# Layer 0's key layer norm: factor and shift on ScalarE in place of two-scalar instructions on VectorE, from the second quarter of keys on

## The chip, the core and the metric

The kernel runs on one core of one Trainium2 chip, in one launch. The core has five engines that work through queues of their own, each in order: TensorE (PE; its weight loads are shown as PEld), VectorE (DVE), ScalarE (ACT), GpSimd (POOL) and SyncE (SP), which here only issues DMAs. ACT issues some DMAs too. An instruction that has to wait holds up everything behind it on its engine. The metric is the device time of one execution in microseconds (us); lower is better.

## The reference, cut to what matters

The model has four blocks (a cross attention and a feed-forward net each) over `x`, 32 batches of 64 tokens of width 128, with a context `ctx_1024` of the same shape. The change lies in the first attention, layer 0, which has 16 heads of width 64:

```python
def _L0_xattn_ref(image_embeds, latents, ln1_g, ln1_b, ln2_g, ln2_b, Wq, Wkv, Wo):
    x = layer_norm(image_embeds, ln1_g, ln1_b)
    l = layer_norm(latents, ln2_g, ln2_b)
    q = l @ Wq
    kv_in = jnp.concatenate([x, l], axis=1)
    k, v = jnp.split(kv_in @ Wkv, 2, axis=-1)
    ...
    w = softmax(einsum('bhqd,bhkd->bhqk', q * scale, k * scale))
    ...
x = x + _L0_xattn_ref(ctx_1024, _layernorm(x, axis=-1), L0_xattn_ln1_g, ...)
```

Each batch has 128 keys: 64 context tokens and 64 latent tokens. A context row is normalised once; a latent row twice in a row, which the kernel does with one mean and one combined factor.

## The kernel before

**Layer 0.** The 32 batches are worked off in eight quarters `q` of four batches. `l0_load` (line 389) brings the keys of a quarter into a tile `kv_tok` of 128 partitions (rows 0 to 63 context, 64 to 127 latents) by four batches by 128, with one DMA on SP's queue and one on ACT's. There are two such buffers, so the load of quarter q+2 waits until quarter q has let go of its own.

`l0_inputs` (line 392) makes the keys ready. DVE takes mean and variance of every row (bn_stats and bn_aggr, lines 154 and 155) and adds the epsilon (lines 398 and 399, 64 rows each); POOL raises the result to the power -1/2 (line 161, tile `ln_rstd`); DVE applies it in place, one instruction of 128x128 for each of the four batches, with mean and factor as two per-partition scalars (`ln_apply`, line 183); then gain and bias rows are multiplied and added over the whole tile (lines 403 and 404), for quarter 0 on DVE and for the others on POOL. PE transposes the result (line 408), ACT copies it out of PSUM as `kvT` (line 409), and DVE and POOL split `kvT`'s latent half and `kv_tok` into a high and a low part (`latT`, `tokp`, lines 213 and 218).

`l0_project` (line 416) multiplies a quarter's latents with the folded query-key matrix A, in eight steps `n` of six matmuls (line 236); ACT copies each out as G (line 425). Its PSUM tag `g` has one bank. `l0_unit` (line 428) is the attention of one batch and eight heads: scores (line 445), maximum and subtraction on DVE (447, 451), exponential on ACT (452, or 456 in every eleventh), sum on DVE (453), reciprocal (460), scaling on POOL (461), transposes on PE (465), copies as high and low part (`pT_hi` on ACT, line 468; `pT_lo` on DVE, 469), the product with the keys (line 236) into `Ct` (ACT, line 473), and after the last unit of a 128-token tile the output product with N (line 479) and the addition to x (DVE, line 480).

**The order of the work.** `interleave` (line 382) runs 64 units with a depth of three, started in turn; between their steps it issues tasks from a list: first `mid_weights`, which loads and prepares weights of the next blocks (among them `w1e` and `w2e`, with large casts on ACT, line 213), then for each finished group of two quarters `mid_group` (layer 0's feed-forward net and layer 1's attention) and the first steps of layer 1's experts. A unit at `n == 0` issues the load of quarter q+2, at `n == 2` its `l0_inputs`. Quarters 0 and 1 are prepared at the start. This is the order of issue; a list scheduler in the compiler then orders each engine's instructions, so a change of one instruction can reorder others. After layer 0, about 320 us into the span, come the experts of layer 1, then layers 2 and 3; nothing of the change is there.

The lines of the change:

```python
    ln_apply(K, tok, tok, mv, rsqrt(K, gp, rs, "ln_rstd"))
    full = [P, GT, P]
    engine = nc.vector if q == 0 else nc.gpsimd
```

Of the kernel before, what the change touches and what calls it, by code (L numbers as in the profile page):

```python
# [23 lines left out]
AF = mybir.ActivationFunctionType  # L24
ALU = mybir.AluOpType
# [5 lines left out]
GT = 4  # L31
# [41 lines left out]
def bank(K, tag, shape, dt=F32):  # L73
    if tag == "c":
        K.cturn = not K.cturn
        tag = "c2" if K.cturn else "c1"
    if tag == "1":
        tag = "c1"
    if tag == "2":
        tag = "c2"  # L80
    return K.ps.tile(shape, dt, tag=tag, name=f"{tag}_ps", bufs=BANKS[tag])
# [65 lines left out]
def ln_moments(K, pool, xg, own=""):  # L147

    nc = K.nc
    n = xg.shape[1]  # L150
    st = pool.tile([P, n, 6], F32, name="ln_st")
    mv = pool.tile([P, n, 2], F32, name=f"ln_mv{own}")
    for t in range(n):
        nc.vector.bn_stats(st[:, t, :], xg[:, t, :])
        nc.vector.bn_aggr(mv[:, t, :], st[:, t, :])
    return mv


def rsqrt(K, pool, v, name):
    out = pool.tile(list(v.shape), F32, name=name)  # L160
    K.nc.gpsimd.tensor_tensor(out, v, K.neghalf.to_broadcast(list(v.shape)), ALU.pow)  # L161
    return out
# [18 lines left out]
def ln_apply(K, out, xg, mv, rstd, after=None):  # L181
    for t in range(xg.shape[1]):
        step = K.nc.vector.tensor_scalar(
            out[:, t, :], xg[:, t, :], mv[:, t, 0:1], rstd[:, t : t + 1], ALU.subtract, ALU.mult
        )
        if after:
            in_turn(K, [after, step])
    return step
# [19 lines left out]
def split(K, pool, src, name, engine=None, bufs=None, after=None):  # L208

    nc = K.nc  # L210
    hi = pool.tile(list(src.shape), F32R, name=f"{name}_hi", bufs=bufs)
    lo = pool.tile(list(src.shape), F32R, name=f"{name}_lo", bufs=bufs)
    first = nc.scalar.copy(hi, src) if isinstance(K, Later) else nc.vector.tensor_copy(hi, src)
    if after:
        in_turn(K, [after, first])
    if not isinstance(K, Later):
        K.mark = first
    (engine or nc.gpsimd).tensor_tensor(lo, src, hi.bitcast(F32), ALU.subtract)
    return hi, lo
# [111 lines left out]
def l0_xattn(K):  # L331
# [3 lines left out]
    with (  # L335
# [8 lines left out]
        with tc.tile_pool(name="first", bufs=1, side="right", reuse_waits="tile") as first:  # L344
# [16 lines left out]
            def take_A(ps, hf, r):  # L361
# [3 lines left out]
                nc.vector.scalar_tensor_tensor(lo, ps, scale, hi.bitcast(F32), ALU.mult, ALU.subtract)  # L365

            l0_inputs(K, C, 0)
            for hf in range(2):
                l0_products(K, take_A, w["WqT"], w["WkT"], hf)
                for n in range(4 * hf, 4 * hf + 4):  # L370
                    l0_project(K, C, 0, n, "gn"[n % 2])
            l0_inputs(K, C, 1)

            with tc.issue_after(K.projected.ins):
# [17 lines left out]
def l0_inputs(K, C, q):  # L392

    nc, gp = K.nc, C.gp
    tok = C.tok[q]
    mv = ln_moments(K, gp, tok)
    rs = gp.tile([P, GT], F32, name="ln_rs")
    nc.vector.tensor_scalar(rs[0:S, :], mv[0:S, :, 1], EPS, None, ALU.add)
    nc.vector.tensor_scalar(rs[S:P, :], mv[S:P, :, 1], 1.0 + EPS, EPS * EPS, ALU.mult, ALU.add)
    ln_apply(K, tok, tok, mv, rsqrt(K, gp, rs, "ln_rstd"))  # L400
    full = [P, GT, P]
    engine = nc.vector if q == 0 else nc.gpsimd
    engine.tensor_tensor(tok, tok, K.kv_gamma.unsqueeze(1).to_broadcast(full), ALU.mult)
    engine.tensor_tensor(tok, tok, K.kv_beta.unsqueeze(1).to_broadcast(full), ALU.add)
    kvT = gp.tile(full, F32, name="kvT", bufs=3)
    ps = bank(K, "1", full)
    for b in range(GT):
        nc.tensor.transpose(ps[:, b, :], tok[:, b, :], K.ident)
    nc.scalar.copy(kvT, ps)
    latp = split(K, gp, kvT[:, :, S : 2 * S], "latT", nc.vector)  # L410
    tokp = split(K, gp, tok, "tokp", bufs=3)
    C.keys[q] = (kvT, latp, tokp)
# [15 lines left out]
def l0_unit(K, C, q, t, hf, b):  # L428
# [8 lines left out]
    if n == 2 and q + 2 < 8:  # L437
        l0_inputs(K, C, q + 2)
# [941 lines left out]
def in_turn(K, steps):  # L1380

    for a, b in zip(steps, steps[1:]):
        order = mybir.DependencyInfo(mybir.DependencyClass.NoSync, mybir.DependencyReason.DATA)
        K.tc.add_manual_dep(b.ins, a.ins.name, order, reason="order of issue")
# [354 lines left out]
```

## Time and profile before

| what | value |
|---|---|
| median of 3 runs | 907.06 us (906.3 to 908.6) |
| the profiled execution | 907.62 us |
| its span | 905.9 us, 1.7 us less |
| mean granted TensorE clock | 0.98 |
| PE busy | 821.4 us (91%) |
| weight loads busy | 671.2 us (74%) |
| DVE busy | 732.4 us (81%) |
| ACT busy | 563.0 us (62%) |
| POOL busy | 328.3 us (36%) |

The profile is that of one execution. Its page gives busy time by engine, then the span in 40 equal slices of 22.6 us with the busy share of each in tenths, and the costliest groups of instructions. Further views are asked of its trace: busy time by window, what an engine waited for (put down to the instruction that came last), the instructions that read or write one tile, groups by form (shapes and operands), a timeline, and the chain of waits that ended last. Starts are counted in us from the start of the span. An instruction's duration reaches into that of its successor on the same engine, so the distance of two starts is less than the duration. The start of the span to about 18 us is loading and the first quarter; there PE has little to do.

### The profile page before, as it was taken

Reading aid. Unit: us, or ns where it says so; the run is one execution under the profiler, and the core shown is the slowest. Engines: PE = TensorE matmul, PEld = TensorE weight load, DVE = VectorE, ACT = ScalarE, POOL = GpSimd, SP = SyncE. Lnnn points to the kernel's source line nnn. Section 1 sums busy time; section 2 is a strip of 40 time slices with the busy share of each in tenths; the row PEclk is TensorE's granted clock in tenths of the full one; section 3 lists DMA queues with packets and bytes.
Section 4 is the critical chain, followed back from the end, with each engine's and each line's share of the span. In section 5 each row is a group of like instructions: output and inputs, shape, how many; then the busy total and the mean of one; then the engine's idle time right before and its main releaser. Section 6 shows DMA issues by size and latency. Waiting matters only on the chain.

```text
span 905.9 us, 15766 instructions
## 1 busy us (share of the span) xinstructions
PE 821.4 (91%) x5859; PEld 671.2 (74%) x5868; DVE 732.4 (81%) x1877; ACT 563.0 (62%) x1093; POOL 328.3 (36%) x300
## 2 busy tenths in 40 slices
PE   4999999999999988899999799898999779898995
PEld 3989989979988876787787688684676447566663
DVE  5879799798698687877678877789788778789878
ACT  3676685676676599587687768564544484345443
POOL 3764574343243251511040310015474303435342
PEclk9999999999999999999999999999999999899998
DMA  8312000000000000000000000000000000000000
GB/s 191 106 36 59 13 2 12 13 1 1 13 1 1 1 13 0 15 14 21 1 1 1 1 1 1 0 25 1 1 2 1 1 1 1 1 1 1 13 13 24
DMA packets 22670, 13.73 MB, mean 15 GB/s; under 512 B 3009, under 2 KB 21953, under 8 KB 22593
## 3 DMA queue, kind: packets, MB, share of 16 engines
q1 hardware_dynamic: 18320, 10.62, 4.3%
q10 hardware_dynamic: 4272, 2.10, 0.9%
q8 instruction: 46, 0.75, 0.3%
q14 instruction: 32, 0.25, 0.1%
HBM read 11.66 MB, written 1.05 MB: 14 GB/s over the span
## 4 chain that ended last, share of the span: by engine, by line
PE 50%; DVE 25%; ACT 15%; POOL 3%; issue 3%; DMA 2%; SPq 1%; ACTq 0%; DVEq 0%; POOLq 0%
PE c_ps L918 7%; PE g_ps L479 4%; PE s_ps L1263 4%; PE s_ps L445 4%; PE g_ps L236 4%; PE c_ps L236 3%; PE g_ps L1283 2%; PE c_ps L1273 2%; PE s_ps L236 2%; PE t_ps L465 2%; PE t_ps L236 2%; ACT L941 2%; DVE mh_lo L895 1%; ACT L936 1%; DVE m L893 1%
## 5 line engine op out<-in xcount | busy, mean ns | idle before, releaser
L461 POOL TENSOR_TENSOR e<-e,rs 128x512 f32<-128x512 f32 x64 | 67.0, 1058 | 91.7 <-DVE rs L460 52.8
L161 POOL TENSOR_TENSOR ln_rstd<-ln_rs,neghalf 128x4 f32<-128x4 f32 (+1 forms) x38 | 40.8, 1073 | 144.8 <-DVE ln_rs L169 137.5
L1249 POOL TENSOR_TENSOR kb<-hk,head 128x1024 f32<-128x1024 f32 x32 | 63.7, 1993 | 74.2 <-PE s_ps L1263 58.9
L445 PE MATMUL s_ps<-kvT,G 128*128 128x128 f32 x512 | 71.7, 277 | 0.5 <-DVE e L451 0.5
L1263 PE MATMUL s_ps<-kb,hq 128*128 128x512 f32 x128 | 67.3, 609 | 2.1 <-ACT hq L1232 1.9
L445 PEld LDWEIGHTS s_ps<-kvT,G 128*128 128x128 f32 x512 | 65.8, 192 | 4.1 <-DVE e L451 1.9
L918 PE MATMUL c_ps<-mh_hi,w2e_hi 128*128 128x512 f32 x160 | 61.8, 426 | 4.5 <-ACT be L936 2.7
L479 PE MATMUL g_ps<-N,Ct 128*128 128x128 f32 x512 | 62.1, 276 | 1.1 <-ACT G L425 0.7
L479 PEld LDWEIGHTS g_ps<-N,Ct 128*128 128x128 f32 x512 | 60.1, 192 | 2.5 <-ACT G L425 1.3
L1266 ACT ACTIVATE e<-e 128x1024 f32<-128x1024 f32 x32 | 34.0, 1061 | 40.6 <-DVE e L1265 38.1
L1264 DVE TENSOR_REDUCE nm<-s_ps 128x8 f32<-128x512 f32 x64 | 43.7, 683 | 16.0 <-PE s_ps L1263 15.6
L1274 ACT COPY hpT<-c_ps 128x512 f32<-128x512 f32 x64 | 35.1, 589 | 34.2 <-PE c_ps L1273 33.9
L469 DVE TENSOR_TENSOR pT_lo<-t_ps,pT_hi 128x512 fp32r<-128x512 f32 x64 | 43.4, 683 | 13.5 <-ACT pT_hi L468 11.3
L918 PE MATMUL c_ps<-mh_hi,w2e_lo 128*128 128x512 f32 x160 | 51.9, 401 | 0.0
L895 DVE TENSOR_TENSOR mh_lo<-m,mh_hi 128x1024 fp32r<-128x1024 f32 x32 | 40.4, 1263 | 13.9 <-ACT mh_hi L894 12.9
L473 ACT COPY Ct<-c_ps 128x512 f32<-128x512 f32 x64 | 38.4, 600 | 21.2 <-PE c_ps L236 16.4
L918 PE MATMUL c_ps<-mh_lo,w2e_hi 128*128 128x512 f32 x160 | 49.4, 404 | 0.5 <-DVE mh_lo L895 0.5
L425 ACT COPY G<-g_ps 128x512 f32<-128x512 f32 x60 | 35.9, 598 | 21.4 <-PE g_ps L236 18.0
L452 ACT ACTIVATE e<-e 128x512 f32<-128x512 f32 x56 | 35.4, 638 | 20.8 <-DVE e L451 20.5
L1283 PEld LDWEIGHTS g_ps<-hv,hpT 128*64 128x64 f32 x1024 | 33.5, 137 | 19.3 <-issue 7.4
L447 DVE TENSOR_REDUCE nm<-s_ps 128x4 f32<-128x512 f32 x64 | 42.9, 679 | 5.0 <-PE s_ps L445 4.7
L468 ACT CAST pT_hi<-t_ps 128x512 fp32r<-128x512 f32 x64 | 38.1, 598 | 13.3 <-PE t_ps L465 7.3
(524 smaller groups left out, 2651.8 us busy)
## 6 DMA issues: line engine op xcount, KB each, us to landing
kv_tok<-in_x ACTq DMA_DIRECT2D x8, 128.0 KB, 3.3
kv_tok<-in_ctx SPq DMA_DIRECT2D x8, 128.0 KB, 2.9
x<-in_x SPq DMA_DIRECT2D x4, 256.0 KB, 8.3
ctx<-in_ctx SPq DMA_DIRECT2D x4, 256.0 KB, 3.4
w2e_raw<-in_L_ffn_expert_w SPq DMA_DIRECT2D x1, 768.0 KB, 4.4
out<-x SPq DMA_DIRECT2D x3, 256.0 KB, 2.3
WkT<-in_L_xattn_WkT ACTq DMA_DIRECT2D x2, 256.0 KB, 5.3
WqT<-in_L_xattn_WqT SPq DMA_DIRECT2D x2, 256.0 KB, 5.2
```

Source lines behind the costliest of these rows:

```text
L236: step = K.nc.tensor.matmul(ps, w[a], x[b], start=start and i == 0, stop=stop and i == 2)
L445: nc.tensor.matmul(ps[:, j, :], G[:, bb, h : h + 2, :].rearrange("p h s -> p (h s)"), kvT[:, bb, :], start=True, stop=True)
L447: K.mark = nc.vector.tensor_reduce(nm, ps, AX.X, ALU.max, negate=True)
L461: nc.gpsimd.tensor_tensor(e, e, rs.unsqueeze(2).to_broadcast([P, 4, P]), ALU.mult)
L469: nc.vector.tensor_tensor(lo, ps, hi.bitcast(F32), ALU.subtract)
L479: nc.tensor.matmul(ps, Ct[:, h, :], C.N[:, h, :], start=(h == 0), stop=(h == 15))
L895: nc.vector.tensor_tensor(lo, m, hi.bitcast(F32), ALU.subtract)
L918: nc.tensor.matmul(ps, K.w2p[part][:, 2 * n + i, cols], x[:, i, :, :], start=first, stop=last)
L1249: step = nc.gpsimd.tensor_tensor(kb, K.hk[C.i][g][:, :, t, :].unsqueeze(2).to_broadcast(full), K.head.unsqueeze(1).unsqueeze(3).to_broadca ...
L1263: nc.tensor.matmul(ps, hq[:, half, t, :, :].rearrange("p b s -> p (b s)"), kb[:, half, :, :], start=False, stop=True)
L1264: nc.vector.tensor_reduce(nm[:, heads], ps, AX.X, ALU.max, negate=True)
L1283: values = nc.tensor.matmul(po[b * S : (b + 1) * S, j, :, :].rearrange("p r d -> p (r d)"), pT[:, j, b * S : (b + 1) * S], K.hv[g][:, 2 * ...
```

## The change

For the quarters 1 to 7 the layer norm of the keys is written as a factor and a shift: (x - m) r = r x + (-m r). DVE computes the shift, one instruction of 128x4, into the tile that held the variances; ACT applies factor and shift, one activation of 128x128 for each of the four batches, with both as per-partition columns. Quarter 0 keeps its instructions.

```diff
-    ln_apply(K, tok, tok, mv, rsqrt(K, gp, rs, "ln_rstd"))
+    rstd = rsqrt(K, gp, rs, "ln_rstd")
+    if q == 0:
+        ln_apply(K, tok, tok, mv, rstd)
+    else:
+
+        shift = rs
+        nc.vector.scalar_tensor_tensor(shift, mv[:, :, 0], -1.0, rstd, ALU.mult, ALU.mult)
+        for t in range(GT):
+            nc.scalar.activation(tok[:, t, :], tok[:, t, :], AF.Identity, bias=shift[:, t : t + 1], scale=rstd[:, t : t + 1])
     full = [P, GT, P]
     engine = nc.vector if q == 0 else nc.gpsimd
```

So 28 of the 32 instructions of line 183 on `kv_tok` leave DVE, seven small ones come to it, and 28 activations come to ACT. ACT now waits for DVE's shift, and POOL's multiplication with the gain waits for ACT where it waited for DVE. No DMA is added or taken away; those that wait for a `kv_tok` buffer keep their places in the queues of SP and ACT.

## The prediction

> **What bounds the kernel now.** I read the page's busy slices first, to see which engine fills the stage of the change; layer 0 with the keys' layer norm is the first third, slices 1 to 14.
>
> ```profile
> PE   4999999999999988899999799898999779898995
> DVE  5879799798698687877678877789788778789878
> ACT  3676685676676599587687768564544484345443
> ```
>
> TensorE is at 9 from slice 2 to slice 15, VectorE at 7 to 9, ScalarE at 6 or 7. Then the table of windows: start and end, length, then busy us and instructions of PE, its weight loads, DVE, ACT and POOL, granted clock, DMA share, GB/s.
>
> ```profile
> 18.00:60.00 42.00, 40.68 (x282) 37.04 (x283) 34.51 (x94) 26.61 (x58) 30.08 (x24) 1.00 0.29 86
> 60.00:120.00 60.00, 58.50 (x456) 54.59 (x454) 51.00 (x134) 38.90 (x81) 31.05 (x30) 1.00 0.10 28
> 120.00:180.00 60.00, 59.60 (x473) 56.56 (x474) 49.52 (x133) 39.52 (x88) 27.27 (x25) 1.00 0.04 10
> 180.00:320.00 140.00, 134.66 (x1041) 123.07 (x1041) 112.35 (x301) 92.33 (x191) 48.67 (x46) 1.00 0.02 5
> ```
>
> From 18 to 180 us, where all the moved instructions lie, PE is busy 158.8 of 162 us at full granted clock. DVE is busy 135.0 and ACT 105.0, so ACT has room of 57 us. Pipelined matmuls cover each other's tails, so I asked the waits of the weight-load queue for what PE really stands still for (18 to 320 us; total, times, longest).
>
> ```profile
> PEld g_ps L236 <- DVE latT_hi L213: 3.5, 1, 3.5
> PEld g_ps L236 <- ACT G L425: 2.7, 6, 1.0
> PEld c_ps L236 <- ACT Ct L473: 2.6, 6, 1.3
> PEld s_ps L445 <- DVE e L451: 1.9, 5, 0.8
> PEld g_ps L479 <- ACT G L425: 1.3, 3, 0.9
> PEld c_ps L236 <- DVE pT_lo L469: 0.6, 1, 0.6
> ```
>
> The first is the start, ahead of the changed code. Of the rest of that answer, the lines released by DVE add up to 3.9 us, 2.3 of them before 180 us; the lines released by ACT to 10.5. PE in this stage waits more for evictions by the half-idle ACT than for the busy DVE, because ACT works its queue in order and each eviction is short and urgent. That decides my sign.
>
> **What goes from DVE.** Line 183 on kv_tok, 28 of its 32 instructions.
>
> ```profile
> L183 DVE TENSOR_SCALAR kv_tok<-kv_tok,ln_mv,ln_rstd x32: 319/340/1302, 7.4 to 154.4; 128x128 f32<-128x128 f32 x32
> 91.17 1.83 DVE L183 TENSOR_SCALAR kv_tok<-kv_tok,ln_mv,ln_rstd 128x128 f32<-128x128 f32 x4 [0.52 <-POOL ln_rstd L161]
> 93.66 0.50 PE L236 MATMUL c_ps<-pT_lo,tokp_hi 128*128 128x512 f32 x1 [0.38 <-DVE pT_lo L469]
> ```
>
> In the timeline, the seven runs of four start at 17.97, 24.34, 32.86, 41.92, 91.17, 124.24 and 153.65 us and last 1.12, 2.07, 1.91, 1.11, 1.83, 1.10 and 1.11 us: 10.3 us. A quiet run takes 1.11; the three long ones lie beside POOL instructions. In exchange comes one 128x4 scalar_tensor_tensor a quarter, absent from the trace; its nearest rows are the 64x4 tensor_scalar of line 399 (166 to 1043 ns, median 167) and the 128x4 reciprocal of line 460 (0.17 us). I take 0.17, so 1.2 us in all (7.3 at the worst). DVE is 9.1 us lighter, between 3.0 and 9.5.
>
> How much reaches PE? The chain of waits names kv_tok on DVE twice, at 17.97 and at 91.17. But at 91.17 a delay of 1.83 us cost PE 0.38 us (last line above): PE had other units' matmuls to do. The most that relief can give directly is all of the 2.3 us; I take half, 1.2. The wait for POOL's rstd does not go: the shift needs it too, on the same queue, with reductions and subtractions behind it (0.52 us in the line above, 3.0 us in four waits in all).
>
> **What ACT gets.** 28 activations of 128x128, SBUF to SBUF, with two per-partition columns, not in this form in the trace. Nearest rows by form, busy us and mean ns after the bar:
>
> ```profile
> L818 ACT ACTIVATE hr<-c_ps,cols 128x128 f32<-128x128 f32 x2 | 0.7, 368 | 0.0
> L602 ACT ACTIVATE c<-n_ps,c 128x512 f32<-128x512 f32 x3 | 2.1, 690 | 0.5 <-PE n_ps L600 0.5
> L583 ACT ACTIVATE y<-n_ps,cols 128x512 f32<-128x512 f32 x12 | 9.7, 807 | 0.0
> L229 ACT ACTIVATE ws_raw<-ws_raw 128x128 f32<-128x128 f32 x1 | 0.3, 293 | 0.0
> ```
>
> Line 818 has one column: 368. Line 583 has two, line 602 one, at equal size: a second column costs 117. So 485 ns each. Back to back they overlap by about 0.11 us (copies of 0.58 start 0.47 apart, from 42.97 to 43.43), so a run of four takes 3 x 0.375 + 0.485 = 1.61 us, and 28 take 11.3. Bounds: the row without columns, 293, gives 4 x 0.18 = 0.73 us a run; no overlap gives 1.94. I keep 1.61, since the column rows are the nearer kind. It is half as long again as the quiet DVE run it replaces.
>
> What is queued behind each run I read from the order of instructions of the two builds: in quarters 1, 2 and 5 a copy of G comes directly behind it (in quarter 2 the run is split in pairs around such copies), in 3 and 7 a pT_hi and then a G, in 4 the w1e_raw negation and then a G, in 6 an activation of the middle group. G's PSUM tag g has one buffer, so PE's next group of line 236 waits for that copy, and the exponentials and pT_hi further back hold up DVE. ACT idles 35% from 60 to 180 us, so a run of 1.61 us falls by 0.56 into idle time and pushes what follows by 1.05. PE has a group of 0.7 to 0.9 us to do before it needs the bank and the copy takes 0.6: cover of 0.2. So 0.85 us passes to PE where an eviction stands close behind, which I count for five of seven runs: 4.3 us. With the bounds: five times (0.47 - 0.2) = 1.4, and seven times (1.26 - 0.2) = 7.4.
>
> The new wait, ACT for the shift, is worst in quarter 2: its statistics wait for a load that lands at 21.45, its rstd ends at 24.3, and behind the first pair on ACT stands the G copy that ran at 23.06. It could run at about 25.1. PE loses little, since the N-products of line 326 and transposes fill the gap; I count that as one of the five. POOL's gamma and beta of quarter 1 move from behind DVE's run to behind ACT's; its second pass comes behind quarter 2's rstd instead of ahead of it, so quarter 3's two loads (on SP's and ACT's queues, waiting for that buffer) start some 3 us later than 25.59. Quarter 3's projections run tens of us later; I cost this at nothing, and at 1 us if a DVE wait for that load reaches PE. Order of issue differs up to PE row 669 of 2473 (middle group 2, about 315 us); after that it is the same but for one swapped pair, so what layer 0 wins or loses is carried to the end.
>
> **A rule against the change, and one for it.** The traced rows above have ACT dearer than DVE (1.61 estimated against 1.11). The Trainium skill, "ScalarE: Activation LUTs", section "Rules for kernel authors", tells authors to put adds and multiplies on VectorE, not ScalarE. By those rows and engine time alone the change loses 3.5 us (7 x 0.5), which is less than the 4.3 I count. On the other side the three runs beside POOL took 1.83 to 2.07 instead of 1.11. The skill's "GPSIMD Engine Reference", section "Specifications", says that GpSimd's SBUF interfaces are shared with VectorE and that DVE instructions in a two-port mode contend. By the quiet row alone the relief would be 7.8, by all seven it is 10.3. No run here yet shows whether ACT escapes it.
>
> **Sum.** The profiled execution took 907.62 (span 905.9 and 1.7 around it), 0.56 above the median of 907.06. 907.62 + 4.3 - 1.2 = 910.7 for such an execution, 910.1 for a median; I say 910.0. Bounds of this case in medians: 907.06 + 1.4 - 2.3 = 906.2 to 907.06 + 7.4 = 914.5.
>
> **Rivals.**
> *Relief reaches PE* (faster). ACT's room of 57 us swallows the runs; PE gets back the 2.3 us, and the freed DVE lets the middle groups' chains start earlier, so that part of PE's waits from 180 to 320 us goes: they total 11.8 us in that view, of which I give up to half. 907.1 - 2.3 = 904.8 down to 898.9; I name 902. For it: DVE has 10 of 20 us of the chain in 80:100 and in 180:200. Against it: no kv_tok on DVE after 155 us, and the 0.38 us above. It decides where less than 0.3 us a run passes to PE.
> *PE hides both* (the move does nothing to the end): 906 to 908.5. For it: PE at 59.6 of 60 us. Against: ACT's 10.5 us of holds.
> *The rearranged start collides.* The later quarter 3 loads and the weights w1e and w2e, whose large casts sit in ACT's queue among evictions (w2e_hi 1.47 us at 55.33, Ct behind it), meet the runs; each held Ct delays a 1.8 us group of line 479: 8 to 12 us over, 915 to 919.
>
> **Chances.** A measurement of this kernel tells about 0.3% (2.7 us) from no change: 904.3 and 909.8 are the limits. Forecast 0.45 (0.31 slower, 0.14 within); relief 0.27 (all faster); hiding 0.14 (within); collision 0.14 (slower). Slower 0.45, same 0.28, faster 0.27. Leaving out the lower 0.08 of the relief and the upper 0.06 of the collision, with its highest bound, the range is 900 to 916. The forecast's own range is 906.2 to 914.5.
>
> **What would show it.** Right: ACT rows of about 0.49 us in kv_tok, ACT some 10 us and DVE minus 9 us in 18:180, PE's waits on ACT's G and Ct grown from 10.5 us by some 4, DVE's from 3.9 to under 3, layer 0's last output about 3 us later. Wrong: runs on ACT that lie wholly in its idle time, waits on ACT no longer than before, or a PE that is done with layer 0 earlier. A row under 0.3 us would fail the price; a large difference after 320 us, the carrying.

## The result, and the profile after

The kernel after took 911.39 us (median of 22 executions, 905.96 to 916.73), the kernel before, run on the same chip between them, 906.84 us (22, 903.74 to 911.9). The ratio is 1.0051, with a 95% interval of 1.0037 to 1.0064: slower by 4.5 us. The profiled execution after took 908.46 us (span 906.7), 0.84 more than that of before, at nearly the same mean granted TensorE clock (0.981 and 0.980).

One number has to be known before the others are read. In this study the time follows the granted clock: within the kernels, fitted together, 4.3 us less for each 0.01 more of mean clock (two of the smaller sets, of eight executions each, show little of it). The 22 executions after had a mean clock of 0.9761. The 22 of before that were run between them have no clock on record; the 98 of before that have one, run beside the experiments, had 0.9789. At a common clock of 0.978 the means are 910.7 and 907.5 us. So, as an estimate from these figures, about 3.2 us of the 4.5 belong to the change, and about 1.2 to a lower clock, the reason of which these runs don't show. I give both kinds of numbers below.

The busy slices of the page after:

```profile
PE   4999989999999997899999799998999878898995
DVE  4779879798689767867678787788887788979878
ACT  3786775666766589596677777564544575445443
```

PE still stands at 9 nearly all through layer 0. The windows, with the columns as before (busy us and instructions of PE, weight loads, DVE, ACT, POOL):

```profile
18.00:60.00 42.00, 39.19 (x281) 35.60 (x281) 31.43 (x85) 30.49 (x73) 27.67 (x26) 1.00 0.30 86
60.00:120.00 60.00, 59.22 (x462) 55.29 (x461) 51.43 (x132) 42.17 (x87) 30.07 (x27) 1.00 0.10 28
120.00:180.00 60.00, 56.67 (x435) 51.77 (x434) 46.62 (x119) 39.78 (x91) 27.97 (x26) 1.00 0.03 10
180.00:320.00 140.00, 135.92 (x1052) 124.26 (x1051) 113.59 (x299) 92.33 (x191) 50.43 (x47) 1.00 0.01 3
```

The third line tells where the time went. Up to 120 us PE does 743 instructions (738 before); from 120 to 180 it does 435 (473 before) and is busy 2.9 us less. The weight loads' waits from 18 to 320 us (total, times, longest) name what stands there now:

```profile
PEld g_ps L236 <- DVE latT_hi L213: 3.5, 1, 3.5
PEld s_ps L453 <- DVE e L459: 3.1, 6, 0.9
PEld g_ps L236 <- ACT G L433: 3.1, 7, 1.0
PEld s_ps L453 <- ACT e L464: 2.6, 2, 1.5
PEld n_ps L588 <- ACT y L591: 2.1, 2, 1.9
PEld c_ps L236 <- ACT Ct L481: 2.0, 5, 1.0
```

Those released by ACT add up to 13.5 us (10.5 before), those by DVE, without the start, to 5.0 (3.9 before). Of the 10.5 before, only 3.8 lie ahead of 180 us, where the moved instructions are; there they have grown to 7.4. What has grown is not the copies: all lines of G and Ct together fell from 7.6 to 5.7 us (18 to 320 us). Two other lines are new among the large ones: `e` of line 464, the exponential of every eleventh unit (0.2 before, on line 456), and `y` of line 591, layer 0's feed-forward net in middle group 0 (0.7 before).

A ruler makes it sharper, if it is read with care: the starts of the 16 additions to x (line 480, now 488), one for each output tile of layer 0. In the table, starts in us in the profiled executions.

| output tile | 1 | 2 | 5 | 6 | 7 | 8 | 16 |
|---|---|---|---|---|---|---|---|
| before | 59.73 | 72.25 | 124.04 | 141.65 | 163.60 | 177.41 | 320.56 |
| after | 59.17 | 72.50 | 123.22 | 146.56 | 169.95 | 182.08 | 323.37 |
| after minus before | -0.6 | +0.3 | -0.8 | +4.9 | +6.4 | +4.7 | +2.8 |

Five of the seven runs on ACT are over before tile 5, and PE is 0.8 us ahead. Then, within one tile, 5.7 us go, and some of that comes back later. Not all of it is lost: another order also puts other work ahead of a tile. Up to tile 6 PE does 951 matmuls where it did 940, and is busy 127.25 us where it was 125.73; up to tile 16 it does 2289 in both. Nor does the first half of a microsecond count: the kernel q6_act below has the work and the order of before until tile 5 and reaches tile 1 at 60.31. The moved instructions, duration in ns (shortest/median/longest):

```profile
L408 ACT ACTIVATE kv_tok<-kv_tok,ln_rs,ln_rstd x28: 477/488/562, 18.8 to 148.2; 128x128 f32<-128x128 f32 x28
L406 DVE SCALAR_TENSOR_TENSOR ln_rs<-ln_mv,ln_rstd x7: 130/153/1218, 18.3 to 146.8; 128x4 f32<-128x4 f32 x7
```

ACT's timeline in the bad stretch (start, duration):

```profile
117.76 0.59 ACT L481 COPY Ct<-c_ps 128x512 f32<-128x512 f32 x1
123.21 0.59 ACT L481 COPY Ct<-c_ps 128x512 f32<-128x512 f32 x1 [4.86 <-PE c_ps L236]
...
128.83 1.70 ACT L408 ACTIVATE kv_tok<-kv_tok,ln_rs,ln_rstd 128x128 f32<-128x128 f32 x4
130.38 0.83 ACT L590 ACTIVATE a<-n_ps,half_cols 128x512 f32<-128x512 f32 x1
131.04 0.83 ACT L591 ACTIVATE y<-n_ps,cols 128x512 f32<-128x512 f32 x1
```

and PE's at its end:

```profile
131.92 0.50 PE L588 MATMUL n_ps<-c,w 128*128 128x512 f32 x1 [1.66 <-ACT y L591]
```

ACT stands idle for 4.86 us, because PE does 30 output products in a block ahead of the product it waits for. Then everything is there at once, and ACT works from 123.21 to 139 us without a gap. Quarter 6's run stands in that backlog, behind an exponential and ahead of the second pair of group 0's affine activations, and PE waits for that pair. Two things came together here: the run, and an order of issue with this backlog in it. The first experiments ask which of them costs the time.

### The profile page after: what moved, and what is told of

It reads as the page before. It is cut to its first block, busy times and chain, and to the rows that moved or that the text cites. A ratio compares the mean times of both kernels' runs of the same rounds, so it can differ in the third digit from the quotient of the medians.

```text
span 906.7 us, 15777 instructions
## 1 busy us (share of the span) xinstructions
PE 820.8 (91%) x5859; PEld 669.9 (74%) x5868; DVE 731.0 (81%) x1856; ACT 572.9 (63%) x1121; POOL 324.8 (36%) x300
## 4 chain that ended last, share of the span: by engine, by line
PE 47%; DVE 26%; ACT 17%; issue 3%; POOL 3%; DMA 3%; SPq 0%; ACTq 0%; DVEq 0%; POOLq 0%
PE c_ps L926 6%; PE g_ps L487 5%; PE s_ps L453 4%; PE s_ps L1271 4%; PE c_ps L236 3%; PE g_ps L236 3%; PE c_ps L1281 2%; PE g_ps L1291 2%; PE t_ps L473 2%; ACT L949 2%; PE s_ps L236 2%; DVE m L901 1%; DVE mh_lo L903 1%; ACT L944 1%; DVE nm L1272 1%
## 5 line engine op out<-in xcount | busy, mean ns | idle before, releaser
L971 POOL TENSOR_TENSOR be<-be 128x256 f32<-128x256 f32 x16 | 16.9, 1056 | 81.2 <-DVE tg L976 80.6
```

## The experiments

### First set: the run of quarter 6, or the order

Theory A: quarter 6's run, in ACT's queue among the eight 0.8 us activations of middle group 0, costs the loss between tiles 5 and 6. Theory B: the new order of issue costs it. Four kernels were run.

**q6_pin.** The run of quarter 6 is held back in ACT's queue until behind the last affine activation of group 0.

```diff
+            run = nc.scalar.activation(...)
+            if q == 6:
+                in_turn(K, [K.y_step, run])
...
+        if g == 0:
+            K.y_step = affine
```

> The changed kernel, with quarter 6's four activations held back until the last affine activation of middle group 0 (an order of issue on ACT; PE's and ACT's orders are else those of the changed kernel up to there). Theory A, the run itself, standing in ACT's queue among the group's eight 0.8 us activations, costs the 5.7 us between the fifth and sixth output tile (123.22 and 146.56 us in the changed kernel, 124.04 and 141.65 before): then the 1.66 us wait of PE for the y activation goes, the sixth tile comes at 145 or earlier, the sixteenth at 322 or earlier (323.37 changed, 320.56 before), and the time falls by 1.5 to 3 us. Theory B, the new order of issue of the whole stage (output products in one block of 3.35 us, then 16 us of ACT work in one pile) costs it: the sixth tile stays within 1 us of 146.6, because the pile is the same length, and the time stays within 0.2% of the changed kernel's.

909.47 us, ratio to before 1.0036 (1.0017 to 1.0054), 910.1 at the common clock; tile 6 at 146.64. With the run out of the way of the activations tile 6 comes no earlier, as B said, though nine more matmuls stand ahead of it here (960). But the waits did what A said: PE's wait of 1.66 us for `y` shrank to 0.15, and from 123 to 150 us the weight loads wait 0.6 us on that line where they waited 2.1. So the place of the run holds PE up by 1.5 us there, and not by the 5.7. (The run itself comes later here, at 136.45, and with it the keys of quarter 6.)

**q6_act.** The kernel before, with quarter 6 alone on ScalarE (`if q != 6: ln_apply`). The planner's order stays near that of before.

> The kernel before, with the change made for quarter 6 alone. PE's and ACT's orders are those of before up to the middle group's activations (PE row 354, ACT row 136), and the run of four stands between the group's first and second pair, as in the changed kernel. Theory A (the run in that place): fifth tile at 124.0 as before, sixth at 144 to 147, the sixteenth 2 to 4 us late, time 909 to 911. Theory B (the order before it): sixth tile at 141.7 to 143.2 (no more than the run's own 1.6 us), the sixteenth within 1.5 us of 320.56, time 906 to 908.

908.88 us, ratio 1.0020 (1.0007 to 1.0034). Against before, tile 2 is 0.6 us late (72.82), tile 6 1.5 (143.12), tile 16 1.6 (322.15). So in this order the run costs about 1 us between tiles 2 and 6, not 5. Tiles 6 and, nearly, 16 are where B put them; the time lies between the two forecasts.

**q6_dve.** The kernel after, with quarter 6 back on VectorE (`if q in (0, 6): ln_apply`).

> The changed kernel with quarter 6 kept on DVE as before; PE's and ACT's orders are those of the changed kernel up to the run (ACT row 147). Theory A: fifth tile at 123.2, sixth at 141 to 142.5, sixteenth at 318 to 320.6, time 904 to 907: the other six runs cost nothing. Theory B: sixth tile at 145 or later, time 909 or more. If the forecast's term holds for the other runs (0.85 us each from runs in front of G copies), the fifth tile would be late, which it already isn't.

902.79 us, ratio 0.9955 (0.9936 to 0.9975): faster than both kernels. Tile 6 at 144.04, tile 16 at 317.81. The loss went and 4 us more with it, which neither theory had said; tile 6 lies between the two forecasts. But its order of issue differs from that of the kernel after as well, from about 130 us on to the end of the span, so it doesn't say what it seems to say.

**no_apply.** The kernel before without the 28 applications, with a 128x4 shift and a 128x4 addition in their place; it leaves the application of the norm out for quarters 1 to 7, so it was meant to show the relief alone.

> The kernel before without the four instructions that apply the layer norm of the keys in quarters 1 to 7 (left out; a 128x4 shift and a 128x4 addition stand in their place, so that the chain of waits stays): DVE's relief with no work for ACT. If relief reaches PE, as the rival of the prediction had it, 899 to 905. If PE hides it (PE's waits on DVE in 18 to 180 us were 2.3 us): the sixteenth tile between 318 and 321, time 904.5 to 907.

905.92 us, ratio 0.9994 (0.997 to 1.0018); tile 16 at 315.14, 5.4 us earlier, though a part of the start ran at a lower clock (0.77 from 10 to 20 us). At the common clock the time is 905.7: 1.8 us less than before. Tile 16 is earlier than either forecast had it, the time is as it was forecast for a relief that PE hides. This kernel's order of issue differs from that of before as well, in layer 0 and behind it, so neither the 5.4 nor the 1.8 us is the relief alone. Where the rest of the 5.4 us goes after layer 0 stays open.

The set had one lesson: each of these edits moves the list scheduler to another order, and I had compared orders as much as edits.

### Second set: work and order taken apart

So I wrote the whole order of one kernel down, for all five engines, and gave it to another. Every instruction but the moved ones gets an order dependency (no wait) on its predecessor in the list; the moved ones find a place between, which is still the scheduler's choice. ("Work" is where the norm is applied; "order" is the order of issue of everything else. The added lines shift the numbers: line 408 is 412 in these kernels.) In the traces all instructions of PE, ACT, DVE and POOL but the moved ones do stand in the order that was given.

```diff
+def as_listed(K):
+    shifts = json.loads(zlib.decompress(base64.b64decode(ORDER)))
+    steps = [i for i in list(K.nc.cur_bb.bb.instructions) if i.opcode not in UNLISTED and i.name not in K.moved]
+    for engine, by in zip(("PE", "DVE", "Activation", "Pool", "SP"), shifts):
+        mine = [i for i in steps if str(i.engine).endswith("." + engine)]
+        listed = [mine[n + shift] for n, shift in enumerate(by)]
+        in_turn(K, [SimpleNamespace(ins=i) for i in listed])
```

Theory O says the order costs the time, theory W the moved work.

> The norm's application stands on ScalarE as in the kernel after, but all other instructions of all five engines are issued in the order of the kernel before. Theory O (the order of issue that came with the change costs the time): output tile 6 at 140 to 142 us instead of 146.6, output tile 16 at most at 321, time 905 to 908. Theory W (the moved work itself costs it, wherever it stands): tile 16 at 323 or later, time 909 to 912. In between, with tile 6 at 142 to 144 and 908 to 909: each has a share, as the run of quarter 6 alone on ScalarE suggested (908.9).

> The mirror image: the norm's application stays on VectorE as in the kernel before, but all other instructions are issued in the order of the kernel after. Theory O: tile 6 at 144 us or later (2.4 us or more over 141.65), tile 16 at 322 to 323.5, time 909 to 912. Theory W: tile 6 at 142 or earlier, tile 16 near 320.5, time 906 to 908.

> The work of the version that left quarter 6 on VectorE too (902.8 us), in the order of issue of the kernel before. If its gain comes from work that leaves VectorE, tile 16 stays near 317.8 us and the time at 902 to 904.5. If it comes from the order of issue that the planner gave it, tile 16 goes back to 320 or later and the time to 906 to 908.

> The work of the kernel before (all applications on VectorE), in the order of issue of the version that left quarters 0 and 6 on VectorE. If the gain of that version comes from the order, 902 to 904.5 and tile 16 near 318 us. If it comes from the moved work, 906 to 909 and tile 16 at 320 or later.

With two later runs that fill the square,

> The work of the kernel after (quarter 6 on ScalarE too) in the order of issue of the version that leaves quarters 0 and 6 on VectorE: against that version's 902.8 us only the four applications of quarter 6 differ. If quarter 6's run by itself is worth about 1 us, as it was in the order of before (tile 6 1.1 us later than without it), 903.5 to 905 us and tile 16 near 319. If the run is what costs the kernel after its 4.5 us, 907 or more. If the order alone decides, 902.8 within 1.

> The work of the version that leaves quarters 0 and 6 on VectorE, in the order of issue of the kernel after: against the kernel after only quarter 6's four applications differ, and nothing else changes its place. If quarter 6's run in ScalarE's backlog of 124 to 138 us is the part of the loss that matters, tile 6 comes 3 to 5 us earlier (142 to 143.5), tile 16 at 318.5 to 320.5 and the time is 906 to 908.5. If the order of issue costs it whoever does quarter 6, tile 6 stays at 145.5 or later, tile 16 at 322.5 to 323.5 and the time at 910 to 912. In between, each has its share.

the nine cases are (median us; ratio to before with its 95% interval; mean at clock 0.978):

| work | order of before | order of after | order of q6_dve |
|---|---|---|---|
| all on DVE (before) | 906.9; 1; 907.5 | 910.97; 1.0043 (1.0029 to 1.0057); 910.6 | 905.55; 0.9984 (0.9969 to 1.0); 904.5 |
| quarters 1 to 7 on ACT (after) | 910.57; 1.0036 (1.0021 to 1.0051); 910.2 | 911.39; 1.0051 (1.0037 to 1.0064); 910.7 | 908.50; 1.0012 (0.9996 to 1.0027); 906.0 |
| all but quarters 0 and 6 on ACT (q6_dve) | 908.53; 1.0027 (1.0008 to 1.0045); 909.6 | 908.77; 1.0011 (0.9992 to 1.0029); 909.2 | 902.79; 0.9955 (0.9936 to 0.9975); 902.6 |

The standard error of a mean at the common clock is 0.1 to 0.4 us. More than that comes from the chip: the experiments were run on four chips, and before, which was run beside them on each, has 907.5 us at the common clock on two, 906.7 on the chip of work_after_order_q6dve and 908.3 on that of work_q6dve_order_after. So a difference that has one of these two cells in it is also given against before on the same chip (the kernel after against the mean of all), and differences under 1 us don't count.

The profiles of the nine cases, starts in us. The last column is the start of PE's matmul 2257, near the end of layer 0: with it PE has begun the same 2257 matmuls in all of them, whatever the order.

| work, order | tile 1 | tile 5 | tile 6 | tile 16 | matmul 2257 |
|---|---|---|---|---|---|
| before, before | 59.73 | 124.04 | 141.65 | 320.56 | 316.68 |
| after, before | 61.24 | 126.01 | 144.76 | 323.45 | 319.57 |
| q6_dve, before | 61.87 | 126.72 | 144.32 | 323.20 | 319.32 |
| before, after | 59.78 | 123.89 | 146.07 | 325.49 | 321.62 |
| after, after | 59.17 | 123.22 | 146.56 | 323.37 | 319.50 |
| q6_dve, after | 59.21 | 123.12 | 145.23 | 322.32 | 318.44 |
| before, q6_dve | 59.86 | 124.20 | 145.54 | 320.01 | 317.91 |
| after, q6_dve | 59.70 | 123.44 | 148.24 | 322.45 | 320.35 |
| q6_dve, q6_dve | 59.23 | 122.71 | 144.04 | 317.81 | 315.71 |

Chaining costs nothing by itself that these profiles show: with the work of after until tile 5 and its order, the chained kernel (q6_dve, after) is within 0.1 us of the kernel after at tiles 1 and 5.

Against the forecasts: the work of after in the order of before came as theory W had it (tile 16 at 323.45, 910.6 us), the work of before in the order of after as theory O had it (tile 6 at 146.07, 911.0 us). The six quarters lose their gain in the order of before, as was said of a gain that comes from the order, but come out slower than forecast. The order of q6_dve with nothing moved lies between its two forecasts in time (905.6 us) and has tile 16 where the theory of the work put it (320.01). The work of after in that order has the time of a dear run as measured (908.5 us), but less at the common clock (906.0). The work of q6_dve in the order of after lies between its two forecasts in all three numbers.

The rest of this set is in numbers at the common clock. *The order alone, with the work of before,* costs 3.1 us (order of after) or gains 3.0 (order of q6_dve). The 3.1 are lost inside layer 0: matmul 2257 starts 4.9 us later, of which a lower clock can explain 1.7. The 3.0 are not won there: in the order of q6_dve that matmul starts 1.2 us later than before. By these profiles, one for each case, they come behind layer 0, where this order is another one too and where nothing of the change is. *The work alone, in the order of before,* costs 2.7. Both together cost 3.2, not 5.8. Neither O nor W is the whole story; both are half of it, and they don't add.

*The moved work has no price of its own.* The six quarters 1 to 5 and 7 cost 2.1 us in the order of before (909.6 - 907.5) and gain 1.4 and 1.9 in the two orders that were planned with them (2.2 and 1.8 when each is set against before on its chip). In the old order the loss begins at once: tile 1 starts at 61.24 instead of 59.73, of which up to 0.6 can be the start. There ACT's queue has a fixed place for quarter 2's run, ahead of the copies of G, and stands still for its statistics:

```profile
23.82 0.59 ACT L423 COPY kvT<-c_ps 128x512 f32<-128x512 f32 x1 [0.94 <-PE c_ps L422]
25.90 0.49 ACT L412 ACTIVATE kv_tok<-kv_tok,ln_rs,ln_rstd 128x128 f32<-128x128 f32 x1 [1.49 <-DVE ln_rs L410]
```

The copy of G behind that run starts at 27.45; in the kernel before it started at 26.27. In its own order the kernel after, which splits the run around such copies, has tile 1 at 59.17.

*Quarter 6's run costs 0.6, 1.5 and 3.4 us* in the three orders (last two rows of the table of times; the last two become 2.3 and about 4 when each cell is set against before on its chip). In the order of after the profiles show the way of it in one line. From 123 to 150 us the weight loads wait for `y` with quarter 6 on ACT so:

```profile
PEld n_ps L588 <- ACT y L591: 2.1, 2, 1.9
```

and with quarter 6 on DVE so:

```profile
PEld n_ps L594 <- ACT y L597: 0.6, 2, 0.4
```

The 1.5 us are a wait for what stands behind the run in ACT's own queue, the activation of the middle group. q6_pin had shown the same.

The dearest case goes another way. In the order of q6_dve, with quarter 6 on DVE, POOL's queue runs so:

```profile
126.87 1.68 POOL L411 TENSOR_TENSOR kv_tok<-kv_tok,gains 128x512 f32<-128x512 f32 x1 [1.32 <-DVE kv_tok L183]
128.50 1.04 POOL L469 TENSOR_TENSOR e<-e,rs 128x512 f32<-128x512 f32 x1
```

and with quarter 6 on ACT, in the same order, so:

```profile
130.82 1.26 POOL L417 TENSOR_TENSOR kv_tok<-kv_tok,gains 128x512 f32<-128x512 f32 x1 [4.54 <-ACT kv_tok L412]
132.04 1.04 POOL L475 TENSOR_TENSOR e<-e,rs 128x512 f32<-128x512 f32 x1
```

with PE's weight loads behind that, first with quarter 6 on DVE, then on ACT:

```profile
129.60 0.42 PEld L473 LDWEIGHTS t_ps<-ident,e 128*128 128x128 f32 x4 [0.73 <-POOL e L469]
133.13 0.42 PEld L479 LDWEIGHTS t_ps<-ident,e 128*128 128x128 f32 x4 [3.54 <-POOL e L475]
```

DVE could do quarter 6 as soon as its factor was there. ACT reaches it only at 129.04, behind the backlog. POOL waits 4.54 us for it, the scaling of an attention unit stands behind the gain in POOL's queue, and PE waits 3.54 us for that scaling where it waited 0.73. Here the run doesn't hold up PE through what stands behind it on ACT; it arrives late, and holds up a third engine's queue. In the kernel after, the scheduler has put that scaling ahead of the gain (it runs at 127.41), and only the 1.5 us behind the run on ACT remain.

### Third set: is it one stretch of the order?

Two kernels have the work and the order of after, but one stretch of the order on PE, ACT, DVE and POOL is that of before: the 88 matmuls before tile 5 is added (so the block of 30 output products is split again), and the 99 after that.

> The work and the order of issue of the kernel after, except for one stretch on PE, ScalarE, VectorE and GpSimd (88 of PE's matmuls, the last ones before output tile 5 is added), which goes back to the order of before: the output products in two blocks of eight with the first products of middle group 0 between them, and the first affine pair of middle group 0 ahead of an exponential on ScalarE. If this stretch of the order holds the loss, output tile 6 starts at 142 to 144 us instead of 146.6, tile 16 at 319 to 321.5 and the time is 906 to 909. If it does not, tile 6 stays at 146 or later, tile 16 at 323 and the time at 910 to 912.

909.63 us, ratio 1.0034 (1.0022 to 1.0046), 910.6 at the common clock; tile 5 at 125.86, tile 6 at 147.65. The block of output products and ACT's idle 4.86 us, which looked like the cause in the timeline, are not: without them tile 5 is later and nothing is gained. (Both kernels of this set ran on the chip where before has 906.7.)

> As the run before, but the stretch that goes back to the order of before is the next one (the 99 matmuls from there to the products of output tile 6; quarter 6's transposes then stand behind the output products again). If this stretch holds the loss, tile 6 at 142 to 144 us and the time 906 to 909; if the first one does, tile 6 stays at 145.5 or later and the time at 910 to 912. If neither of the two brings tile 6 under 145, the loss is not in the order of one stretch.

913.28 us, ratio 1.0074 (1.0061 to 1.0087), 912.8 at the common clock. Tile 6 came at 144.76, although 1.7 us of clock were lost from 120 to 130 us in that profile (granted 0.83), so the stretch does bring tile 6 earlier, with 940 matmuls ahead of it instead of 951; but tile 7 is at 173.11, 3.2 us later than after, 1.7 of them the clock. What one stretch gives, the next takes back.

So the order's 3.1 us can't be put down to one of these two stretches. Which property of the order holds them stays open.

### Tiles and clock in these profiles

Five of the profiles had a shortfall of granted clock inside layer 0, worth 1.7 us of PE time each time it shows (0.83 in a window of 10 us), and 3.4 at the start (0.83 from 10 to 30 us): work_before_order_after at 150 to 160 us, q6_pin at 200 to 210, order_stretch_2 at 120 to 130, work_after_order_q6dve at 130 to 140 and at the start, and no_apply, as said, at the start. Tile 16 starts in these at 325.49, 325.65, 326.89, 322.45 and 315.14 us; without the shortfall the first three would be near 323.8, 323.9 and 325.2, if PE loses all of it. This is why the table of times goes by many executions, and tiles of one execution are read only against neighbours.

The clock is not wholly apart from the kernel, though. The four shortfalls behind the start began at 152.0, 205.7, 125.6 and 134.5 us, and beside each PE had stood still: 1.00 us ahead of 150.32, 1.39 ahead of 204.61, 2.59 ahead of 125.98, 3.11 ahead of 133.13. Not every such wait has one beside it (the 1.66 us ahead of 131.92 in the kernel after has none). So a kernel's own waits may lower its clock, and the 1.2 us that I put down to the clock in the result may in part belong to the change; no run here separates the two.

## Why the prediction was right, and where its steps were not

It said 910.0 us, range 900 to 916, slower as the likeliest; measured were 911.4, or 910.7 at the common clock. The sum (4.3 lost on ACT, 1.2 won on DVE, 3.1 net) met the 3.2 us at the common clock almost exactly. That was luck: its parts did not meet.

- **PE is the bound: held. Its waits on ACT's copies grow: not so.** The waits on ACT rose from 10.5 to 13.5 us where 4 more were foreseen, but the prediction looked for them at G and Ct, and these fell from 7.6 to 5.7 (the 10.5 that it gave them was all of ACT). The growth is in `y` and in exponentials. The comparison behind the sign was uneven as well: 2.3 us of waits on DVE ahead of 180 us were set against 10.5 on ACT up to 320, of which 3.8 lie ahead of 180. The waits on DVE were to fall under 3 and rose to 5.0.
- **The price on ACT: held.** 485 ns were estimated, the median is 488; a run of four takes 1.63 to 1.70 us (1.61 estimated; quarter 2's, split in pairs, apart); ACT is busy 11.7 us with all 28 (11.3).
- **What leaves DVE, 9.1 us: mis-sized.** From 18 to 180 us DVE is busy 5.6 us less (135.0 to 129.5). The applications gave back 9.2 (14.65 to 5.49 for line 183), but the seven shifts took 3.0, not 1.2. Five took 0.13 to 0.16 us; the two that fell beside a POOL instruction (24.37 beside one of 24.31, 91.55 beside one of 91.49) took 1.22 and 1.00 and ended with it. Other short DVE instructions lengthened as well (the 26 of `ln_rs<-ln_mv` until 335 us from 5.8 to 10.1 us in all). The delay beside POOL went over to the small instructions that stayed. Of the 28 activations on ACT none took over 562 ns, against 1302 for the same work on DVE. The Trainium skill, "GPSIMD Engine Reference", section "Specifications", says that GpSimd's SBUF interfaces are shared with VectorE; these durations agree with it, and ACT's rows show no such delay.
- **"0.85 us passes to PE where an eviction stands close behind, which I count for five of seven runs": this step failed.** The five runs that were over by tile 5 cost nothing in the order that came with the change: tile 5 is at 123.22, and in the same order with all of them on DVE at 123.89. (In the order of before they do cost, 2.0 us by tile 5, and there a copy of G is held behind quarter 2's run.) One of the two runs that I had set apart, quarter 6 with "an activation of the middle group" behind it, stood where the loss arose. The 1.5 us that its run costs there are a wait for just that activation: the mechanism showed there, and that place was counted at nothing. In another order the same run costs more through what waits for its result on a third engine (POOL's gain, and the scaling behind that); of that queue the prediction had not asked.
- **The order of issue, counted as 0: this step failed too.** I read the new order as a list of neighbours, and for how far it goes (in the traces, but for one swapped pair, to 240 us, not 315). That another order has a price by itself, 3.1 us with the work of before, was in no term. The rival of the colliding start came nearest in kind, but it put the collision at the start, where the new order loses nothing (tile 1 at 59.17, before at 59.73) and in fact saves most of the 1.5 us by which tile 1 is late with quarter 2's run in the old one.
- **The quarter 2 wait, counted as one of the five runs at 0.85 us: less, by the scheduler's doing.** ACT waits 4.0 us in two waits for the shift, and tile 2 is 0.3 us late.
- **The carrying: held.** Tile 16 was to be 3 us late and was 2.8; at the common clock the time is 3.2 longer. It holds because this order is the old one again behind layer 0; in the order of q6_dve, which is not, some 4 us change behind it.
- **The rival that relief reaches PE** (902) did not come about in the kernel after, but the relief is not sized. The kernel without any application is 1.8 us faster at the end; at matmul 2257 it is 3.6 us ahead (313.04), more than the 2.3 that the prediction allowed, and both figures hold another order too. That 902.8 was measured with six quarters moved is due to work and order together: that order gives 3.0 with nothing moved, by its profile behind layer 0, and the six quarters 1.9 more.

So the total was right with wrong parts that made up for each other: five runs that cost nothing were counted at 4.3 us, and an order that cost some 3 us and quarter 6's run, which cost 1.5 or more, at nothing.

A version faster than both kernels came out of it: quarters 0 and 6 on VectorE, the others on ScalarE, 902.8 us, 0.9955 (0.9936 to 0.9975) of before. In its profile 1.0 us of that is won by matmul 2257; the larger part comes behind layer 0, from the other order there.

## What to carry to other kernels

Where a scheduler places the instructions, an edit is two changes, the work and a new order, and each can be worth as much as the other; the order can be held fixed by chaining every instruction to its predecessor in a written list, and only then does the time of an edit tell the price of the work. Work that goes to an engine with idle time is priced by when that engine's queue reaches it, by what stands behind it there at that moment, and by what stands behind its consumer on a third engine, not by the share of busy time. Before a gain is believed, run the old work in the new order, and compare progress at a point where both orders have done the same work.

## What the runs showed of the hardware that was not expected

- The time of one kernel varies with the granted clock by more than the change: 905.96 to 916.73 us after, correlation -0.96 with the mean clock of the execution (0.963 to 0.985). One kernel also differs from chip to chip: before has 906.7 to 908.3 us at the common clock on the four chips of the experiments.
- ACT's recorded durations grow through an unbroken stretch of work while the distance of starts stays: in q6_dve the affine activations take 0.80 us at 124.34 and 0.96 at 134.29, started 0.67 to 0.68 us before their successors both times; after idle gaps the record is short again (0.78 at 270.38, behind 0.56 us of idle time). So in these records the duration in a dense stretch overstates the price, and the distance of starts is the better measure.
